# Four graph layers in fp32: where the next group's H and 1/D, single additions and output-projection products stand around layer 1's attention

## The chip, the cores and the metric

The kernel runs on one core of a Trainium2 chip. The metric is the device time of one execution, in microseconds. Below, PE is TensorE (matmul), DVE is VectorE, ACT is ScalarE, POOL is GpSimd and SP is SyncE, which issues most of the DMAs.

## The reference

The input x holds 128 graphs of 64 nodes with 512 features, adj holds their weighted adjacency matrices. Four layers follow each other; each adds its result to x and normalizes the rows.

```python
# layer 0: hypergraph convolution twice, 512 -> 1024 -> 512
H = (adj != 0); w = adj[:, 0, :]
Dinv = 1 / (H @ w);  Binv = 1 / H.sum(axis=1)
conv(z, W, b) = Dinv * (H @ (Binv * (H^T @ (z @ W^T)))) + b
x = LN(x + conv(layer_norm(relu(conv(x, W1, b1))), W2, b2) + x)
# layer 1: attention from one score per node
s = (x @ w) @ a
A = leaky(8 * tanh((s_i + s_j) / 8)); A = exp(A) * adj
A = A / A.sum(-1) * adj.sum(-1)
x = LN(x + A @ x @ w)
# layer 2: three graph convolutions; layer 3: attention with 8 heads
x = LN(x + adj @ (relu(adj @ (relu(adj @ (x @ gW1) + gb1) @ gW2) + gb2) @ gW3) + gb3)
x = LN(x + heads(softmax(q k^T / 8) * LA + LG * adj + LD * exp(-adj), v) @ Wout + b_out)
```

## The kernel before, in words

**Groups and pairs.** Two graphs fill the 128 partitions and make a pair; G = 4 pairs make a group of 512 rows, and there are 16 groups. All is fp32. A matmul of 128x256 appears twice in the profile for each one in the program.

**Products.** `multiply` (L546) makes a product of 512 rows by 512 columns by Strassen's way (in Winograd's form) with seven products of half size instead of eight. `product` (L528) issues one of them: 8 matmul records, or 16 where the inner size is 1024 (layer 0's W2). Their order is B11, T1, T2, B21, T3, B22, T4. B11, T2, T3 and T4 accumulate in the PSUM tile `pa` (in the profile a_ and the product's key: a_l2c, a_wo), T1 and B22 in `pc` (b_l2c, b_wo), B21 in `pb` (c_l2c, c_wo). After B11, T1 and T2 a copy of the sum so far is taken (`snap`, L555: u1, u5 and u2, all shown as u_l2c and so on); ACT takes it where there is no residual, DVE where there is one. Four additions make the result: L574 after B21 (quarter 0,0), L580 after T3 (1,1), L589 after B22 (0,1), and L598 (a copy on ACT) or L600 after T4 (1,0). T3 accumulates into `pa`, which the copy u2 reads, and T4 into `pa`, which L580 reads. There are four accumulators of this kind (`ps_acc`, bufs=4), so a new tile takes the place of one that an addition has emptied. `sums` (L514) makes the left sides of the seven products on DVE (s_h, s_l and so on); the differences of weights (T1 to T4) are made once, at group 0 (`make`, L263 to L268), and kept in DRAM.

**A group's stages.** `prepare` (L628) makes H and 1/D of a group: ht (H transposed, L633), its row sums db (L635), hn (L641), deg (L642), rowsum (L643), H times the weights and its sums (L660, L661), the inverses inv (L649 to L651), then rb, 1/D turned along the rows (`along`, one transpose of L618 and four of L622), hb (L670), and with PE's sps the matrix smat; cs (L705) is D times degree. `first_half` (side a) is layers 0 and 1 of a group: products l0w1, graph products l0h, product W2 (l0w2), layer norm, the scores and e (`along` again), t = e + s (L817), tanh (L819), exp (L821), tn (L823), den (L828), its turn rd, t (L832), then the products gt_l of x and t, and l1w. `second_half` (side b, and later t) is layer 2 (l2a, l2b, gth, l2c with the result g3, the aggregation agg, L1138, with its additions L1144, the layer norm and xtp, the turned x) and layer 3 (q, k, dot, v, softmax, pv, wo). `first_group` is group 0's own first half, with plain products by rows.

**Order.** The generators of three groups run interleaved: in step n side a works on group n, side b on group n - 1, t on group n - 2. `order` (L1385) lists the stages of one step by hand, `step_1` is step 1's list, `step_last` step 16's, `start` group 0's. Within that list a scheduler orders each engine's instructions by when it takes them to be ready; in group 0 and at the very end the written order is kept (`strict`). `behind(key)` (L501) ties an instruction behind a noted one on the same engine: `last_add` notes additions (`wo_5.d` is the addition L580 of wo of group 5), PE's products (`l2c_5.p5` is the end of T3) and others (`e_5` is t = e + s, `t_5` the finished t, L832). The program's order on an engine is the order in which it runs there.

**Weights.** `Stream` loads each product's weights into a ring of 20 tiles as earlier ones come free. A group's adj is loaded more than a step ahead.

Of the kernel before, what the change touches and what calls it, by code (L numbers as in the profile page):

```python
# [10 lines left out]
AF = mybir.ActivationFunctionType  # L11
# [30 lines left out]
def kernel(  # L42
# [286 lines left out]
    w_o = Weight(Wout, 0, "wo")  # L329
# [166 lines left out]
    last_add = {}  # L496
# [4 lines left out]
    def behind(key):  # L501
        return tc.issue_after(last_add[key]) if key in last_add else nullcontext()
# [40 lines left out]
                )  # L543
        stream.done(*wt_q, what)

    def multiply(lefts, wt_q, dst, key, flipped=False, res=None, stops=(3,), then=None, held=None):  # L546

        acc = [ps_acc.tile([P, 2, Q], FP, name=f"{n}_{key}", tag="acc") for n in "ab"]

        def snap(ps, m, n, what):
            t = work.tile([P, 2, Q], FP, name=f"{what}_{key}", tag="w")
            last_add[f"{key}.{what}"] = (act.copy(t, ps) if res is None else vec.tensor_add(t, ps, res(m, n))).ins  # L555
            return t

        pa, pc = acc
        product(pa, lefts, wt_q, B11, True, False, flipped)
        s1 = snap(pa, 0, 0, "u1")  # L560
        if 1 in stops:
            yield
        product(pc, lefts, wt_q, T1, True, False, flipped)
        s5 = snap(pc, 1, 1, "u5")
        if 2 in stops:
            yield
        product(pa, lefts, wt_q, T2, False, False, flipped)
        s2 = snap(pa, 0, 1, "u2")
        last_add[f"{key}.p3"] = newest(PE)
        if 3 in stops:  # L570
            yield
        pb = ps_acc.tile([P, 2, Q], FP, name=f"c_{key}", tag="acc")
        product(pb, lefts, wt_q, B21, True, True, flipped)
        vec.tensor_add(dst(0, 0), pb, s1)  # L574
        if then:
            then(0, 0, dst(0, 0))
        if 4 in stops:
            yield
        product(pa, lefts, wt_q, T3, False, False, flipped)
        last_add[f"{key}.d"] = vec.tensor_add(dst(1, 1), pa, s5).ins  # L580
        if then:
            then(1, 1, dst(1, 1))
        last_add[f"{key}.p5"] = newest(PE)
        if 5 in stops:
            yield
        product(pc, lefts, wt_q, B22, False, True, flipped)
        last_add[f"{key}.p6"] = newest(PE)
        with behind(held):
            last_add[key] = vec.tensor_add(dst(0, 1), pc, s2).ins  # L589
        if then:  # L590
            then(0, 1, dst(0, 1))
        if 6 in stops:
            yield
        product(pa, lefts, wt_q, T4, False, True, flipped)
        if then:
            then(1, 0, pa)
        elif res is None:
            act.copy(dst(1, 0), pa)  # L598
        else:
            vec.tensor_add(dst(1, 0), pa, res(1, 0))  # L600

    def whole(gen):
        for _ in gen:
            pass

    def nat(t):

        return lambda m, n: t[:, 2 * m : 2 * m + 2, n * Q : (n + 1) * Q]
# [19 lines left out]
    def prepare(g):  # L628
# [24 lines left out]
        if q == 0:  # L653
            inverse(inv[:, 1], db[:, 1])
        else:
            by_rows()
            if q > 2:
                yield
            with behind(f"agg_{q - 2}") if q > 2 else nullcontext():
                vec.tensor_mul(hn[:, 1], hn[:, 0], g["wb"])  # L660
                vec.reduce_sum(db[:, 0], hn[:, 1], axis=AX.X)  # L661
                inverse(inv, db)
        cs = small.tile([P, G], FP, name=f"cs_{q}", tag="cs")
        g["cs"], g["rowsum"] = cs, rowsum
        if q > 0:

            rb = grp.tile([P, G, C], FP, name=f"rb_{q}", tag="rb", bufs=1)
            along(rb, inv[:, 0])
        hb = grp.tile([P, G, C], FP, name=f"hb_{q}", tag="hb", bufs=1)
        vec.tensor_mul(hb, ht, bcast(inv[:, 1], G))  # L670
        yield
# [64 lines left out]
    def first_half(g):  # L736
# [79 lines left out]
        t = grp.tile([P, G, C], FP, name=f"t_{q}", tag="t", bufs=1)  # L816
        last_add[f"e_{q}"] = vec.tensor_add(t, e, bcast(s4, G)).ins  # L817
        yield "w2"
        act.activation(t, t, AF.Tanh, scale=0.125)  # L819
        vec.scalar_tensor_tensor(t, t, 0.1, t, ALU.mult, ALU.max)  # L820
        last_add[f"exp_{q}"] = act.activation(t, t, AF.Exp, scale=8.0).ins  # L821
        tn = grp.tile([P, G, C], FP, name=f"tn_{q}", tag="tn", bufs=1)
# [73 lines left out]
    def first_group(g):  # L896
# [107 lines left out]
        out_of_2(0, rows_of(0, hts, w2))  # L1004
        yield "w20"
        out_of_2(1, rows_of(1, hts, w2))
        scored(0)
        yield "w21"
        ps = rows_of(2, hts, w2)
        yield "w22"  # L1010
        attention(0)
# [2 lines left out]
        ps = rows_of(3, hts, w2, 0, 1)  # L1014
        yield "w23"
        out_of_2(3, rows_of(3, hts, w2, 1, 2, ps))
        scored(1)
        stream.used(w_2)
        yield "w24"
        left = Left("l1_0")  # L1020
        graph_T(pair, t, left.t, 0, "l1_0")
        yield "c30"
        mvs = [small.tile([P, 2, 2], FP, name=f"mv_l1_0_{d}", tag="mvp") for d in range(2)]

        def out_of_l1(p):
# [29 lines left out]
    def second_half(g):  # L1055
# [62 lines left out]
        h2.sums()  # L1118
        yield "gh"
        g3 = big.tile([P, G, D], FP, name=f"g3_{q}", tag="big")  # L1120
        gen = multiply([h2], (w_g[2], q), nat(g3), f"l2c_{q}", stops=(3, 5), held=f"t_{q + 1}")
        next(gen)
        yield "l2c1"
        with behind(f"e_{q + 1}"):
            next(gen)
        yield "l2c2"
        with behind("exp_1") if q == 0 else nullcontext():
            whole(gen)
        yield "l2c"
        for duo in range(2):  # L1130

# [67 lines left out]
            taken(1, ps, left)  # L1199
        left.sums()  # L1200
        yield "osum"
        for n, _ in enumerate(multiply([left], (w_o, q), nat(xg), f"wo_{q}", res=nat(xg), stops=(1, 3))):
            yield f"o{n + 1}"
        yield "o"
        with behind(f"q_{q + 1}"):
            o = out[q * T : (q + 1) * T, :].rearrange("(p t) d -> t p d", t=P)
# [165 lines left out]
    def taken(duo, ps, left):  # L1372
# [6 lines left out]

    start = """  # L1380
        a0.c1 prep0 keep0 rest a0.w1a keep1 a0.w1b rows0 bw0 a0.c20 wa bw0 a0.c21 doubled0 constant0 rows1 a0.w20 keep2 wa
        a0.w21 prep1 a0.w22 a0.ss0 a1.c1 a0.w23 doubled1 a0.w24 a0.c30 a1.w1a1 a0.l10 a0.ss1 a0.l11 a1.w1a2
        a0.c31 a1.w1a keep3 a1.resid a0.l12 a1.w1b1 a0.l13 a1.w1b2 b0.gt a1.w1b
    """.split()
    order = """  # L1385
        t.v1 a.c1 t.v b.gt t.soft a.w1a1 a.w1a t.soft2 a.resid b.l2a1 b.l2a a.w1b1 t.ptp a.w1b t.pv a.lnh b.l2b1
        t.osum a.c2a b.l2b a.c2b b.gb3 load a.w21 b.gh a.w2 rows b.l2c1 b.l2c2 a.ss a.den b.l2c t.o1 t.o2 a.c3 b.agg rows2 t.o
        a.p1 b.xT a.p2 b.q1 a.ln1 b.q t.ln3 b.k1 prep b.k b.dots
    """.split()

    step_1 = """
        b.l2a1 b.l2a a.lnh b.l2b1 a.c2a b.l2b a.c2b b.gb3 load a.w21 b.gh a.w2 b.l2c1 b.l2c2 a.ss sumsq b.l2c a.den b.agg
        sumsq2 a.c3 a.p1 b.xT sumsk a.p2 b.q1 a.ln1 b.q b.k1 rows b.k prep b.dots
    """.split()

    step_last = """
        t.v1 b.gt t.v t.soft t.soft2 b.l2a1 t.ptp b.l2a t.pv t.osum b.l2b1 b.l2b b.gb3 b.gh b.l2c1 b.l2c2 b.l2c t.o1 b.agg
        t.o2 t.o b.xT b.q1 b.q t.ln3 b.k1 b.k b.dots
    """.split()
    rest_last = "t.v1 t.v2 t.v t.pv0 t.o1 t.pv1 t.o".split()  # L1400
    orders = {1: step_1, NGRP: step_last, NGRP + 1: rest_last}
# [43 lines left out]
    for n, (who, q, name) in enumerate(todo):  # L1445
        if n == n_start:
            strict.clear()
        if n == n_end:
            strict.update((PE, DVE))
        if who == "load":  # L1450
            if q > 1:
                groups[q] = load_group(q)
        elif who == "rows":
            if q > 0:
                preps[q] = prepare(groups[q])
            with behind(f"l0w2_{q - 1}" if q > 2 else "q_0") if q > 1 else nullcontext():
                next(preps[q])
        elif who in ("prep", "rows2"):
            next(preps[q])
        elif who == "doubled":  # L1460
            doubled(groups[q])
        elif who == "constant":
            constant(groups[q])
        elif who == "keep":
            wt = (*w_1, w_2, w_l1)[q]
            stream.keep(wt)
        elif who == "wa":
            if isinstance(wa_parts, tuple):
                wa_parts = make_wa(*wa_parts)
                vec.tensor_copy(mcol, mcol8)  # L1470
                vec.tensor_copy(mi, mi8)
            else:
                spread_wa(wa_parts)
        elif who == "rest":
            with in_turn(SP, POOL):
                wa_parts = load_wa()
                b2_bc = load_row(b2, D, "b2_bc")
                groups[1] = load_group(1)
                load_atx(first)
                load_masks(first)  # L1480
                load_masks_cols()
                gb1_col = load_col(gb1, KD, "gb1_col")
                gb2_col = load_col(gb2, KD, "gb2_col")
                gb3_bc = load_row(gb3, D, "gb3_bc")
                bo_bc = load_row(bout, D, "bo_bc")
        elif who in ("sumsq", "sumsq2"):
            stream.make_half(w_q)
        elif who == "sumsk":
            stream.make(w_k, 0)
        elif who == "bw":  # L1490
            next(bw_parts)
        else:
            side = "a" if who == "a" else "b"
            if (side, q) not in gens:
                gens[side, q] = (second_half if side == "b" else first_half if q > 0 else first_group)(groups[q])
            did = next(gens[side, q])
            assert did == name, (did, name)
# [55 lines left out]
```

## Time and profile before

| | |
|---|---|
| runs | 2763.16 us median of 3 (2761.98 to 2764.21) |
| the profiled execution | 2763.43 us, its span 2761.7 us |
| PE busy | 2726.4 us, 99% |
| DVE busy | 2074.4 us, 75% |
| ACT busy | 801.8 us, 29% |
| share of DMA engines, hardware queue | 46.9% |
| step 3, from b_wo to b_wo (525.0 to 694.8) | 169.8 us, PE busy 168.78, DVE 128.79 |
| group 0 (0 to 140) | PE busy 132.69 |

Busy times overlap and do not add up. In the timeline an entry is start, length, engine, line, operation, output and inputs, shape, count; a bracket at the end is the engine's idle time before it and what ended that. Matmuls overlap each other, so a sum of starts tells more than idle time. The granted clock of TensorE was 1.000.

### The profile page before, as it was taken

To read this page: it belongs to the slowest core of one execution; us is meant where nothing else is said; L and a number is where in the kernel's file an instruction comes from. 1 tells how busy PE (TensorE), PEld (TensorE's weight loads), DVE (VectorE), ACT (ScalarE), POOL (GpSimd) and SP (SyncE) were. 2 spreads that over 40 slices of the span, in tenths; PEclk is the share of its full clock that TensorE was granted. 3 is DMA by queue.
4 is the path that set the end of the run, shared out by engine and by line. 5 is a ranking of instruction groups with operands and counts; after the bars stand their busy time and mean duration, and the time that the engine had idled before them with its cause. 6 is when DMAs were issued, how large, how long until landed. Compare 5 with 4: busy or idle time off the path is not lost.

```text
span 2761.7 us, 67726 instructions
## 1 busy us (share of the span) xinstructions
PE 2726.4 (99%) x28770; PEld 2346.2 (85%) x28770; DVE 2074.4 (75%) x4117; ACT 801.8 (29%) x1444; POOL 37.6 (1%) x71
## 2 busy tenths in 40 slices
PE   9999999999999999999999999999999999999998
PEld 7888888888888888888888888888888888888887
DVE  6878687776877778777786877778777687776766
ACT  3323223233232322322223232232322323132232
POOL 2000000000000000000000000000000000000000
PEclk9999999999999999999999999999999999999999
DMA  8535454454544545445454454545545455454541
GB/s 267 170 116 160 131 164 139 139 164 132 168 130 138 166 133 162 130 142 165 132 164 128 143 164 132 162 127 149 161 130 166 132 153 152 125 164 131 153 124 61
DMA packets 309389, 405.14 MB, mean 147 GB/s; under 512 B 57409, under 2 KB 185185, under 8 KB 309089
## 3 DMA queue, kind: packets, MB, share of 16 engines
q1 hardware_dynamic: 304256, 385.58, 46.9%
q0 software_dynamic: 4832, 15.24, 1.5%
q8 instruction: 228, 3.74, 0.6%
q14 instruction: 73, 0.59, 0.1%
HBM read 369.78 MB, written 30.93 MB: 145 GB/s over the span
## 4 chain that ended last, share of the span: by engine, by line
PE 85%; DVE 13%; issue 1%; ACT 1%; DMA 0%; DVEq 0%
PE a_l0w L539 13%; PE b_l0w L539 7%; PE a_l2b L539 4%; PE a_l2a L539 4%; PE a_v L539 4%; PE c_l0w L539 4%; PE a_k L539 4%; PE a_q L539 4%; PE a_l1w L539 3%; PE gt_l L481 3%; PE a_l2c L539 2%; PE gt_l0h L481 2%; PE a_wo L539 2%; PE b_l2b L539 2%; PE b_l1w L539 2%; PE b_l2a L539 2%
## 5 line engine op out<-in xcount | busy, mean ns | idle before, releaser
L539 PE MATMUL a_l0w<-w2w,aT_l0h 128*128 128x256 f32 x720 | 164.3, 381 | 0.0
L457 DVE BATCH_NORM_STATS2 st_l<-x 128x6 f32<-128x512 f32 x244 | 157.3, 670 | 0.1
L539 PEld LDWEIGHTS a_l0w<-w2w,aT_l0h 128*128 128x128 f32 x720 | 135.6, 190 | 18.8
L463 DVE TENSOR_SCALAR x<-x,mv_l,rs_l 128x512 f32<-128x512 f32 x244 | 119.1, 540 | 1.8
L539 PE MATMUL b_l0w<-w2w,s_l0h 128*128 128x256 f32 x480 | 108.5, 379 | 0.0
L766 ACT ACTIVATE h<-h 128x1024 f32<-128x1024 f32 (+1 forms) x58 | 54.9, 947 | 178.5 <-DVE h L589 157.5
L539 PEld LDWEIGHTS b_l0w<-w2w,s_l0h 128*128 128x128 f32 x480 | 91.1, 190 | 12.5
L1112 ACT ACTIVATE aT_h<-gth,gb_col 128x256 f32<-128x256 f32 x128 | 48.5, 490 | 159.0 <-PE gth L1104 159.0
L447 ACT ACTIVATE rs_l<-mv_l,eps_t 128x4 f32<-128x4 f32 (+1 forms) x64 | 19.0, 297 | 257.6 <-DVE mv_l L458 245.8
L555 DVE TENSOR_TENSOR u_l0w<-a_l0w,b_bc 128x512 f32<-128x512 f32 x56 | 38.5, 688 | 69.3 <-PE a_l0w L539 69.3
L492 ACT COPY aT_l<-gt_l 128x512 f32<-128x512 f32 x148 | 78.2, 597 | 40.0 <-PE gt_l L481 39.9
L539 PE MATMUL a_l1w<-ww,aT_l 128*128 128x256 f32 x360 | 87.3, 379 | 0.2 <-ACT aT_l L492 0.2
L539 PE MATMUL a_l2b<-gwbw,aT_h 128*128 128x256 f32 x360 | 86.6, 383 | 0.7 <-ACT aT_oT L1375 0.7
L539 PE MATMUL a_wo<-wow,aT_oT 128*128 128x256 f32 x336 | 80.7, 383 | 6.1 <-DVE x L580 6.1
L539 PE MATMUL a_q<-aT_xT,wqw 128*128 128x256 f32 x360 | 85.1, 379 | 0.7 <-ACT aT_xT L1163 0.7
L539 PE MATMUL a_l2c<-gwcw,aT_h 128*128 128x256 f32 x360 | 85.3, 380 | 0.0
L539 PE MATMUL a_k<-aT_xT,wkw 128*128 128x256 f32 x360 | 85.0, 379 | 0.0
L539 PE MATMUL a_l2a<-aT_l,gwaw 128*128 128x256 f32 x360 | 85.0, 379 | 0.0
L539 PE MATMUL a_v<-wvw,aT_xT 128*128 128x256 f32 x336 | 80.8, 383 | 0.0
L539 PE MATMUL a_l0w<-w1aw,aT_l 128*128 128x256 f32 x336 | 80.8, 383 | 0.0
L539 PE MATMUL a_l0w<-w1bw,aT_l 128*128 128x256 f32 x336 | 79.4, 379 | 0.0
L539 PEld LDWEIGHTS a_wo<-wow,aT_oT 128*128 128x128 f32 x336 | 62.8, 190 | 19.4 <-DVE x L580 10.9
(528 smaller groups left out, 6491.2 us busy)
## 6 DMA issues: line engine op xcount, KB each, us to landing
w2w<-w2k SPq DMA_DIRECT2D x210, 256.0 KB, 2.7
x<-in_x_dram SPq DMA_DIRECT2D x15, 1024.0 KB, 5.7
w1aw<-w1ak SPq DMA_DIRECT2D x60, 256.0 KB, 2.6
w1bw<-w1bk SPq DMA_DIRECT2D x60, 256.0 KB, 2.7
ww<-wk SPq DMA_DIRECT2D x60, 256.0 KB, 2.7
gwaw<-gwak SPq DMA_DIRECT2D x60, 256.0 KB, 3.0
gwbw<-gwbk SPq DMA_DIRECT2D x60, 256.0 KB, 2.6
gwcw<-gwck SPq DMA_DIRECT2D x60, 256.0 KB, 2.6
```

The costliest lines, as they stand in the source:

```text
L447: act.activation(rs[:, at], mv[:, at, 1], AF.Sqrt, bias=eps_t)
L457: vec.bn_stats(st, xg[:, p, :])
L463: vec.tensor_scalar(xg[:, p, :], xg[:, p, :], mv[:, p, 0:1], rs[:, p : p + 1], ALU.subtract, ALU.mult)
L481: ten.matmul(ps[g][f * C : (f + 1) * C, c, p, :], src(2 * duo + p)[rows, c0 : c0 + C], mat[rows, 2 * duo + p, :], start=True, stop=True,)
L492: act.copy(o[:, :, :, g, :], ps[g])
L539: ten.matmul(acc[:, blk, :], lhsT, rhs, start=(first and blk == 0 and i == 0), stop=(last and i == n_k - 1), skip_group_check=True,)
L555: last_add[f"{key}.{what}"] = (act.copy(t, ps) if res is None else vec.tensor_add(t, ps, res(m, n))).ins
L766: act.activation(hn, hn, AF.Relu)
L1112: act.activation(o[:, :, h, :], ps[h][:, c].rearrange("p (d a) i -> p d (a i)", d=2), AF.Relu, bias=gb2_col[:, k : k + 1],)
```

## The change

- `prepare`: its first part (ht, db, hn, deg, rowsum) is tied behind W2's addition L580 of the group ahead (`l0w2_{q-1}.d`) instead of its last addition, and stands before side b's l2c1 in step 1 too. In group 2 the second part is tied as the first was before. Then comes a stop, and rb is tied behind L580 of the output projection of three groups before (`wo_{q-3}.d`); hb is not tied.
- `multiply`: `held` is now a table. In l2c the addition after B21 is tied behind `e_{q+1}` and the one after B22 behind `t_{q+1}`; before, all that followed the first stop up to T3 was traced behind `e_{q+1}`. In group 0 the tie behind `exp_1` goes, and `a.den` stands before `b.l2c` in step 1.
- Output projection: one stop more (after T1), and its second and third product are tied behind l2c's T3 and T4 of the next group.
- In group 1 the tanh is tied behind l2c's copy u2 of group 0.
- Group 0: `scored(0)` comes after the next group's smat, `scored(1)` after the first graph product of layer 1.

```diff
-    def multiply(..., then=None, held=None):
+    def multiply(..., then=None, held={}):
...
-        vec.tensor_add(dst(0, 0), pb, s1)
+        with behind(held.get(4)):
+            vec.tensor_add(dst(0, 0), pb, s1)
...
-        with behind(held):
+        with behind(held.get(6)):
             last_add[key] = vec.tensor_add(dst(0, 1), pc, s2).ins
...
+        last_add[f"{key}.p7"] = newest(PE)
...
-            if q > 2:
+            if q > 1:
                 yield
-            with behind(f"agg_{q - 2}") if q > 2 else nullcontext():
+            with behind(f"agg_{q - 2}" if q > 2 else "q_0") if q > 1 else nullcontext():
...
+            if q > 2:
+                yield
             rb = grp.tile([P, G, C], FP, name=f"rb_{q}", tag="rb", bufs=1)
-            along(rb, inv[:, 0])
+            with behind(f"wo_{q - 3}.d"):
+                along(rb, inv[:, 0])
...
-        act.activation(t, t, AF.Tanh, scale=0.125)
+        with behind("l2c_0.u2") if q == 1 else nullcontext():
+            act.activation(t, t, AF.Tanh, scale=0.125)
...
         out_of_2(1, rows_of(1, hts, w2))
+        yield "w21"
         scored(0)
-        yield "w21"
+        yield "sc0"
...
-        scored(1)
         stream.used(w_2)
         yield "w24"
...
         yield "c30"
+        scored(1)
+        yield "sc1"
...
-        gen = multiply([h2], (w_g[2], q), nat(g3), f"l2c_{q}", stops=(3, 5), held=f"t_{q + 1}")
+        gen = multiply([h2], (w_g[2], q), nat(g3), f"l2c_{q}", stops=(3, 5),
+            held={4: f"e_{q + 1}", 6: f"t_{q + 1}"})
         next(gen)
         yield "l2c1"
-        with behind(f"e_{q + 1}"):
-            next(gen)
+        next(gen)
         yield "l2c2"
-        with behind("exp_1") if q == 0 else nullcontext():
-            whole(gen)
+        whole(gen)
...
-        for n, _ in enumerate(multiply([left], (w_o, q), nat(xg), f"wo_{q}", res=nat(xg), stops=(1, 3))):
-            yield f"o{n + 1}"
+        gen = multiply([left], (w_o, q), nat(xg), f"wo_{q}", res=nat(xg), stops=(1, 2, 3))
+        next(gen)
+        yield "o1"
+        for n in range(2):
+            with behind(f"l2c_{q + 1}.p{5 + 2 * n}"):
+                next(gen)
+            yield f"o{n + 2}"
+        whole(gen)
...
-            with behind(f"l0w2_{q - 1}" if q > 2 else "q_0") if q > 1 else nullcontext():
+            with behind(f"l0w2_{q - 1}.d") if q > 1 else nullcontext():
                 next(preps[q])
```

In the lists of stages `start` gets a0.sc0 and a0.sc1, `order` gets t.o3 and rows3, `step_1` has rows before b.l2c1, rows2 before b.k1 and a.den before b.l2c, and `step_last` gets t.o3.

## The prediction

> **What bounds the kernel now.** I read the page's first part, then TensorE's (PE's) table of waits, then the timeline around the two longest waits that repeat.
>
> ```profile
> span 2761.7 us, 67726 instructions
> PE 2726.4 (99%) x28770; PEld 2346.2 (85%) x28770; DVE 2074.4 (75%) x4117; ACT 801.8 (29%) x1444; POOL 37.6 (1%) x71
> ```
>
> PE is the bound: 2761.7 - 2726.4 = 35.3 us of the span are not matmul. The change removes no matmul, so only PE's waiting can be won, and any time that DVE saves counts only where PE waits for DVE.
>
> ```profile
> PE b_wo L539 <- DVE g L574: 6.8, 13, 1.1
> PE a_wo L539 <- DVE x L580: 6.6, 13, 0.5
> ...
> PE a_l2c L539 <- ACT u_l2c L555: 1.8, 1, 1.8
> ```
>
> Two waits come 13 times each, once per step 2 to 14 (a step is one turn of the order, about 169.8 us). The first of them, in step 8:
>
> ```profile
> 1372.86 1.89 PE L539 MATMUL b_l2c<-gwcw,s_h 128*128 128x256 f32 x8
> ...
> 1374.15 0.43 DVE L817 TENSOR_TENSOR t<-e,s 128x256 f32<-128x256 f32 x1
> 1374.49 0.68 DVE L574 TENSOR_TENSOR g<-c_l2c,u_l2c 128x512 f32<-128x512 f32 x1
> 1374.61 0.42 ACT L819 ACTIVATE t<-t 128x256 f32<-128x256 f32 x1 [4.83 <-DVE t L817]
> ...
> 1374.93 0.57 ACT L555 COPY u_l2c<-a_l2c 128x512 f32<-128x512 f32 x1
> ...
> 1375.23 1.13 PE L539 MATMUL b_wo<-wow,s_oT 128*128 128x256 f32 x4 [0.48 <-DVE g L574]
> ```
>
> A product of 8 matmuls takes 1.73 us of PE (a_l2c starts at 1371.13, b_l2c at 1372.86). So the next was due at 1374.59; b_wo needs the bank that VectorE's (DVE's) L574 empties, and that addition stands behind L817. It starts 0.64 late and its first four matmuls take 0.97 instead of 0.86, 0.11 more: **0.75 us lost**, though the table of waits calls it 0.48 (overlap of matmuls hides the rest).
>
> ```profile
> 1389.84 1.89 PE L539 MATMUL b_wo<-wow,s_oT 128*128 128x256 f32 x8
> 1389.87 0.45 DVE L618 STREAM_TRANSPOSE rb<-inv 128x256 f32<-128x256 f32 x1
> 1390.24 0.38 DVE L670 TENSOR_TENSOR hb<-ht,inv 128x256 f32<-128x256 f32 x1
> ...
> 1390.64 1.25 DVE L622 STREAM_TRANSPOSE rb<-inv 32x128 f32<-32x128 f32 x4
> ...
> 1391.92 0.69 DVE L580 TENSOR_TENSOR x<-a_wo,u_wo 128x512 f32<-128x512 f32 x1
> ...
> 1392.67 0.48 PE L539 MATMUL a_wo<-wow,aT_oT 128*128 128x256 f32 x1 [0.51 <-DVE x L580]
> ```
>
> The second: a_wo's last product (T4) waits for L580, whose input (T3 of a_wo) was done at 1390.00, but which stands behind the turning of 1/D (rb). Due at 1391.99 after two a_l1w matmuls, it starts at 1392.67, and takes 1.83 instead of 1.73: **0.78 lost**.
>
> Step 15 prepares no further group: H and rb are missing from it, the rest is the same. It is a ready experiment:
>
> ```profile
> 2561.45 1.89 PE L539 MATMUL b_l2c<-gwcw,s_h 128*128 128x256 f32 x8
> ...
> 2562.18 0.42 DVE L817 TENSOR_TENSOR t<-e,s 128x256 f32<-128x256 f32 x1
> ...
> 2562.96 0.57 ACT L555 COPY u_l2c<-a_l2c 128x512 f32<-128x512 f32 x1
> ```
>
> From the start S of b_l2c's second product, L817 begins at S+0.73 here and at S+1.29 in step 8; u_l2c ends at S+2.08 here, S+2.64 there. There b_wo is only 0.08 late, and a_wo's T4 not at all.
>
> **What the Trainium skill says.** "PSUM — Partial Sum Buffer", Engine vs sequencer instructions: ScalarE's (ACT's) and DVE's queues are strict FIFO, matmuls start in program order. The trace agrees: a_l2c's T2 ended at 1373.02, but its copy u_l2c stood behind the tanh until 1374.93. "Perfetto Trace Analysis", Optimization Strategy: the same gap over and over on the saturated engine can mean too few PSUM buffers. It fits the first wait (four accumulators, b_wo needs c_l2c's), not the second. "ScalarE: Activation LUTs", What ACT_TABLE_LOAD costs: 1283 ns, 2.66 us with its drain. The trace has the 1.28 but no drain: in step 8 a load begins at 1398.38, 0.02 after a copy, and the root runs at 1399.67.
>
> **The change, part by part** (order of instructions as the changed program has them, durations from step 8).
>
> *H into W2.* Five DVE instructions (ht 0.28, hn 0.26, db 0.39, deg 0.39, rowsum 0.41: 1.73 in all) go behind W2's addition L580 of the group ahead. In the hole there
>
> ```profile
> 1357.52 0.69 DVE L580 TENSOR_TENSOR x<-a_l0w,u_l0w 128x512 f32<-128x512 f32 x1 [2.76 <-PE a_l0w L539]
> 1360.18 0.69 DVE L518 TENSOR_TENSOR s_h<-aT_h 128x512 f32<-128x512 f32 x1 [1.97 <-PE b_l0w L539]
> ```
>
> they end by 1359.6 (1358.12 plus starts 0.2 to 0.33 apart plus the last's 0.41), so nothing waits; adn and atc are loaded a group ahead. The layer norm behind it then runs as in step 15, 0.56 earlier. Without that cover it would cost up to 1.73.
>
> *Additions and projection products one by one.* PE's order was B22 of l2c, half of b_wo, T3 of l2c; it becomes B22, T3, six matmuls of b_wo, T4, the rest. b_wo no longer stands first; T3 does, and it needs u_l2c, still behind the tanh from step 3 on. With step 15's timing u_l2c ends at S+2.08, PE follows 0.06 later (as at 192.74 in step 1, after a copy that ended at 192.68): T3 at S+2.14, due at S+1.73: 0.41 + 0.10 = 0.51 lost instead of 0.75, **a gain of 0.24**. What is late next: T4 needs the addition L580 of g3, on DVE behind den at S+4.31, done S+5.0; PE comes to T4 at S+2.14 + 0.10 + 1.73 + 6 x 0.216 = S+5.27. It just fits. t is ready at S+7.3, its products come at S+9.2.
>
> *1/D in two parts.* rb and its four blocks go behind L580 of wo; only hb (0.38) stays ahead. L580 then runs from 1390.17 to 1390.86, T4 is due at 1391.57: **the 0.78 are gone**. rb's 1.7 us now lie before the addition L589 at about 1392.55 (1392.53 before); a_l1w and its sums have a slack of 1 us. The next check is the layer norm for xtp (L1158): PE comes 0.78 earlier, at 1402.45; its pairs 0 and 1 are ready at about 1401.6, pairs 2 and 3 at 1402.5 for use at 1403.05. It fits by some 0.5.
>
> *Steps 1 and 2.* Here u_l2c goes ahead of the tanh and T3 does not wait (1.8 + 0.2 won in step 1). But in step 1 g3's addition L589 now stands behind t and one weight difference: t ends at about 196.85, L589 at 198.05; the aggregation, which needs it, then takes 2.6 us, so the next turn comes at 200.7 instead of 199.25: net 1.4 lost. Later H no longer delays kT's addition: the 0.6 wait with its overlap, 0.7, goes. In step 2 four weight differences (0.6 each) move ahead of t; DVE reaches the addition for T4 at S+4.05, T4 waits 1.4, where before b_wo lost 1.2 and more: 0.1 won, and the second wait's 0.78.
>
> *Group 0's two places.* S (smat) ahead of the score takes 0.8 of PE's wait for it (gt_l on smat), aT_l ahead of the root 0.5 (pp on aT_l), with overlap 1.5. The score's root still starts at 86.76, since it waits for statistics that end at 86.73. DVE runs through from there to 98.40 without PE, so W1's next product on a_l0w, due at 98.2, waits 0.3 for the copy that ends then: 1.2 won.
>
> *The queues of DMA.* On SP one adn load changes places with a weight's, which is asked for long before its use; on POOL nothing moves.
>
> *Step 15* loses 0.51 - 0.19 = 0.3 by T3's new place.
>
> **Sum:** -1.2 + 1.4 - 0.7 - 0.9 - 12 x (0.24 + 0.78) + 0.3 = -13.3 us. The profiled execution took 2763.43 (span 2761.7); that gives 2750.1, and against the median of the runs, 2763.16, 2749.9. I say 2750.
>
> **Unknown sizes.** The first wait's gain lies between -0.32 (norm no earlier: u_l2c at S+2.64, 1.07 lost) and +0.75 (no wait); taken 0.24, since step 15 shows that very timing. Over 12 steps this is 2757 to 2744. Steps 1 and 2 together: -3 to +3, taken -0.2.
>
> **Rivals.**
> 1. *The first wait vanishes too*, were u_l2c ready by S+1.67. Step 15 speaks against it. 2744. Chance 0.10.
> 2. *Given back at xtp*: the layer norm behind rb is late and eats the 0.78. For it: DVE is 75% busy. Against: the 0.5 of slack worked out. Then -13.3 + 13 x 0.78 = -3.2: 2760. Chance 0.08.
> 3. *Slower: T3 at the head of PE's queue.* If the tanh's table load falls between t and u_l2c, T3 starts 1.28 later: 1.79 lost instead of 0.75, 0.26 more than the second wait gives back: 12 x 0.26, 1.3 more in step 15 and -1.1 for the ends make about 2766. With the skill's 2.66 a step loses 1.64 net: about 2784. It turns slower once u_l2c ends after about S+3.1. For it: the load stands behind u_l2c in the new steps 1 and 2. Against: from step 3 on ACT's order is as before, the load in 4.83 us of idle time. Chance 0.05.
> That the change does nothing is excluded by the order of instructions.
>
> **How the numbers follow.** The sum's case has 0.77. The range 2744 to 2757 holds it with its bounds and rival 1; rivals 2 and 3 (0.13) are left out. A measurement here tells 0.2%, 5.5 us, from no change: faster 0.88, same 0.08 (rival 2), slower 0.04 (most of rival 3).
>
> **What would show it.** Right: no wait a_wo on x L580; b_wo on g L574 gone, in its place a_l2c on ACT u_l2c some 0.25 each, 13 times; in step 1 agg waiting for g L589 by some 3 us; H's lines ending before s_h. Wrong: a wait xtp on x (rival 2), a_l2c waits above 1 us (rival 3), or none (rival 1).

## Result, and the profile after

The changed kernel took 2749.28 us (median, 2748.92 to 2751.61), the kernel before 2763.53 (2761.98 to 2764.21): a ratio of 0.9951, 95% interval 0.9934 to 0.9968. The prediction said 2750, so the time was right. It was right in the 12 equal steps to a hundredth of a us each, and in the start and steps 1 and 2 by errors that cancel, as shown below.

The head of the page of the changed kernel:

```profile
span 2747.5 us, 67717 instructions
PE 2722.5 (99%) x28770; PEld 2347.5 (85%) x28770; DVE 2079.6 (76%) x4117; ACT 803.3 (29%) x1444; POOL 38.1 (1%) x71
```

The matmuls are as many as before, and what is not matmul fell from 35.3 to 25.0 us (2747.5 - 2722.5). PE's busy time fell by 3.9 as well, since part of a wait is counted as busy there: at T3 below the first matmul after the wait has a record of 0.48 us, the others 0.38.

TensorE's table of waits of the changed kernel (us in total, times, longest):

```profile
PE a_l2c L539 <- ACT u_l2c L555: 3.2, 13, 0.3
PE agg L1145 <- DVE g L590: 2.8, 1, 2.8
PE a_l2c L539 <- DVE g L581: 1.5, 2, 1.0
```

Both waits that came 13 times are gone, b_wo on g and a_wo on x. In place of the first stands a shorter one, T3 of l2c on u_l2c. The aggregation's wait in step 1 is new. Step 8 around T3, from the timeline of the changed kernel (a count at the end covers what lies in the window that was asked for). Line numbers have moved: the additions L574, L580 and L589 are L575, L581 and L590, t = e + s (L817) is L822, the tanh (L819) L825, ht (L633) L635, rowsum (L643) L645, rb's turn (L618) L620, hb (L670) L675, the aggregation (L1138) L1145 and its additions (L1144) L1151.

```profile
1365.64 1.89 PE L539 MATMUL b_l2c<-gwcw,s_h 128*128 128x256 f32 x8
...
1366.37 0.42 DVE L822 TENSOR_TENSOR t<-e,s 128x256 f32<-128x256 f32 x1
...
1366.83 0.42 ACT L825 ACTIVATE t<-t 128x256 f32<-128x256 f32 x1 [4.29 <-DVE t L822]
1367.15 0.57 ACT L555 COPY u_l2c<-a_l2c 128x512 f32<-128x512 f32 x1
...
1367.77 1.56 PE L539 MATMUL a_l2c<-gwcw,aT_h 128*128 128x256 f32 x6 [0.25 <-ACT u_l2c L555]
```

With S = 1365.64: L822 begins at S+0.73, the copy ends at S+2.08, T3 starts at S+2.13. It was due at S+1.73, so it is 0.40 late, and its first matmul takes 0.10 more until the next one starts (0.32 instead of 0.22). That is step 15's timing of before, now in every step. The second place of the same step:

```profile
1382.38 1.89 PE L539 MATMUL b_wo<-wow,s_oT 128*128 128x256 f32 x8
1382.42 0.42 DVE L675 TENSOR_TENSOR hb<-ht,inv 128x256 f32<-128x256 f32 x1
1382.76 0.68 DVE L581 TENSOR_TENSOR x<-a_wo,u_wo 128x512 f32<-128x512 f32 x1
...
1383.36 0.43 DVE L620 STREAM_TRANSPOSE rb<-inv 128x256 f32<-128x256 f32 x1
...
1384.11 1.67 PE L539 MATMUL a_wo<-wow,aT_oT 128*128 128x256 f32 x7
```

L581 ends at 1383.44, 0.67 ahead of T4, where before it ended after T4 was due; rb follows it. And H, in the hole of W2:

```profile
1350.30 0.69 DVE L581 TENSOR_TENSOR x<-a_l0w,u_l0w 128x512 f32<-128x512 f32 x1 [2.76 <-PE a_l0w L539]
1350.91 0.28 DVE L635 TENSOR_SCALAR ht<-atc 128x256 f32<-128x256 f32 x1
...
1351.96 0.41 DVE L645 TENSOR_REDUCE rowsum<-adn 128x4 f32<-128x256 f32 x1
1352.96 0.69 DVE L518 TENSOR_TENSOR s_h<-aT_h 128x512 f32<-128x512 f32 x1 [0.59 <-PE b_l0w L539]
```

The five instructions end at 1352.37, and VectorE still waits 0.59 for TensorE before s_h: the cover held.

The period, from one start of c_wo to the next, is 168.75 to 168.77 us in the repeating steps, against 169.77 before, but for single steps in which PE halts inside a group of small matmuls (the profile calls it "issue"; more of that at the end).

### The profile page after: what moved, and what is told of

Its sections match the earlier page's. It is cut to its first block, busy times and chain, and to the rows that moved or that the text cites. A ratio compares the mean times of both kernels' runs of the same rounds, so it can differ in the third digit from the quotient of the medians.

```text
span 2747.5 us, 67717 instructions
## 1 busy us (share of the span) xinstructions
PE 2722.5 (99%) x28770; PEld 2347.5 (85%) x28770; DVE 2079.6 (76%) x4117; ACT 803.3 (29%) x1444; POOL 38.1 (1%) x71
## 4 chain that ended last, share of the span: by engine, by line
PE 88%; DVE 10%; ACT 1%; issue 1%; POOL 0%; DVEq 0%; POOLq 0%
PE a_l0w L539 13%; PE b_l0w L539 7%; PE a_l2b L539 4%; PE a_q L539 4%; PE a_k L539 4%; PE a_l2a L539 4%; PE a_v L539 4%; PE c_l0w L539 4%; PE a_l1w L539 4%; PE gt_l L481 3%; PE a_wo L539 3%; PE gt_l0h L481 2%; PE a_l2c L539 2%; PE b_l2b L539 2%; PE b_q L539 2%; PE b_k L539 2%
## 5 line engine op out<-in xcount | busy, mean ns | idle before, releaser
L539 PEld LDWEIGHTS b_l0w<-w2w,s_l0h 128*128 128x128 f32 x480 | 91.1, 190 | 12.5
L539 PEld LDWEIGHTS a_l2c<-gwcw,aT_h 128*128 128x128 f32 x360 | 67.0, 190 | 18.7 <-ACT u_l2c L555 8.7
```

Of the source, the lines that this page charges most:

```text
L539: ten.matmul(acc[:, blk, :], lhsT, rhs, start=(first and blk == 0 and i == 0), stop=(last and i == n_k - 1), skip_group_check=True,)
```

## The experiments

The medians are of 4 to 21 executions. The ratios of e1 to e8 are to executions of the kernel before that were timed along with them (median 2763.33). Three further kernels, e9 to e11, are one execution each and stand in the text. The period is that of the undisturbed steps 3 to 14, from one trace of each kernel.

| kernel | median us | ratio to before, 95% | period us |
|---|---|---|---|
| before | 2763.5 | | 169.77 |
| changed | 2749.28 | 0.9951 (0.9934 to 0.9968) | 168.76 |
| e1 H back | 2757.47 | 0.9978 (0.9969 to 0.9986) | 169.32 |
| e2 no product ties | 2745.76 | 0.9937 (0.9924 to 0.9949) | 168.45 |
| e3 rb back | 2760.23 | 0.9988 (0.9982 to 0.9995) | 169.54 |
| e4 g3 free in step 1 | 2747.23 | 0.9942 (0.9928 to 0.9955) | 168.76 |
| e5 before, with H alone | 2756.76 | 0.9975 (0.9965 to 0.9985) | 169.22 |
| e6 group 0 back | 2752.54 | 0.9961 (0.9947 to 0.9974) | 168.77 |
| e7 e2 and e4 together | 2743.24 | 0.9929 (0.9916 to 0.9941) | 168.44 |
| e8 e7, u_l2c early | 2746.16 | 0.9937 (0.9925 to 0.9950) | 168.59 |

**H back in the layer norm** (e1):

```
-            with behind(f"l0w2_{q - 1}.d") if q > 1 else nullcontext():
+            with behind(f"l0w2_{q - 1}" if q > 2 else "l0w2_1.d") if q > 1 else nullcontext():
                 next(preps[q])
```

> The changed kernel with one part undone: from step 2 on, H's five VectorE instructions stand again in the layer norm in front of the first product's addition. Theory (T3's stall is set by u_l2c, behind the tanh, and H's place sets when the tanh comes): L822 begins 0.56 us later after b_l2c's start, T3 of l2c idles about 0.8 instead of 0.25 and loses 1.07 instead of 0.51 in each of 12 steps, the step takes 169.3 instead of 168.8 us, the whole 2749.3 + 12 x 0.56 = 2756. Rival (the gain of the first wait comes from the new order of products and H's place is worth nothing, since H fell into VectorE's idle time before as after): 2749, T3 idle unchanged at 0.25.

In its timeline, step 8, T3 waits 0.80 where it waited 0.25:

```profile
1372.28 1.56 PE L539 MATMUL a_l2c<-gwcw,aT_h 128*128 128x256 f32 x6 [0.80 <-ACT u_l2c L555]
```

The period is 0.56 longer, as the theory had it, so H's place is worth 0.56 a step although H ran on an engine with idle time before and after. The median is 1.5 above the sum. The trace has one more wait in step 2 (gt_l on t, 0.5), and three of its periods are longer than 169.32, by 1.5 in all, where one of the changed kernel's is longer, by 0.5; these are the "issue" halts.

**The projection's products untied** (e2):

```
-            with behind(f"l2c_{q + 1}.p{5 + 2 * n}"):
-                next(gen)
+            next(gen)
```

> The changed kernel with one part undone: the projection's second and third product are no longer tied behind l2c's, so half of b_wo stands again ahead of T3 of l2c; H and 1/D stay at their new places. Theory (with H early, b_wo needs only the bank of c_l2c, which step 15 of the kernel before got 0.08 late, so this order loses 0.19 a step where the tied one loses 0.51): a_l2c's wait on u_l2c goes, b_wo waits 0.1 or less on g, the step takes 168.45 instead of 168.77, the whole 2749.3 - 13 x 0.32 = 2745. The part of the change named 'products tied one by one' would then cost time by itself. Rival (the tie is what removes the first wait): b_wo waits 0.48 again and loses 0.75, the step 169.0, the whole 2752.

The period is 168.45, and a_l2c's wait on u_l2c is gone from the table. Tying the products one by one costs 0.31 a step by itself: it puts T3, which needs the copy u_l2c behind the tanh, ahead of b_wo, which needs only the accumulator that L575 empties, and with H early L575 comes in time. Step 8 of e2:

```profile
1366.02 1.89 PE L539 MATMUL b_l2c<-gwcw,s_h 128*128 128x256 f32 x8
1367.09 0.68 DVE L575 TENSOR_TENSOR g<-c_l2c,u_l2c 128x512 f32<-128x512 f32 x1
1367.83 1.13 PE L539 MATMUL b_wo<-wow,s_oT 128*128 128x256 f32 x4
```

Here S is 1366.02; b_wo starts at S+1.81, 0.08 late, with 0.10 more in its first matmul.

**rb ahead of the projection's addition** (e3):

```
-            if q > 2:
-                yield
             rb = grp.tile([P, G, C], FP, name=f"rb_{q}", tag="rb", bufs=1)
-            with behind(f"wo_{q - 3}.d"):
-                along(rb, inv[:, 0])
+            along(rb, inv[:, 0])
```

(with `rows3` out of the order)

> The changed kernel with one part undone: the turning of 1/D (rb and its four blocks) stands again ahead of the projection's second addition. Theory (the second wait is that turning and nothing else): a_wo waits on x 0.5 us 13 times again and loses 0.78 each, the step takes 169.55 us, the whole 2749.3 + 13 x 0.78 = 2759.4. Rival (part of what the first wait gave is absorbed here, because the second wait is fixed by VectorE's own chain): the second wait grows to 0.78 + 0.24 = 1.02 a step, 2762.6. Other rival (given back at xtp, so that the place of rb is worth less): 2753 or less.

The table of waits of e3 has both:

```profile
PE a_wo L539 <- DVE x L581: 6.6, 13, 0.5
...
PE a_l2c L539 <- ACT u_l2c L555: 3.2, 13, 0.3
```

169.54 - 168.76 = 0.78, neither 1.02 nor less. The second wait does not absorb what the first gives, because VectorE's work ahead of it starts from TensorE's own aggregation (its first addition, L1148 in e3, waits 0.25 for agg; from there to L581 VectorE runs without a break) and so moves with it.

**H alone on the kernel before** (e5). The edit is one word, `.d`, at the place of e1; TensorE's order is that of before.

> The kernel before with one part of the change alone: from group 3 on, H's five VectorE instructions stand behind W2's second addition; TensorE's and ScalarE's orders are those of before. Theory (H in the layer norm is the whole of the first wait except 0.19): b_wo's wait on g falls from 0.48 to 0.1 or less in 12 steps, the step takes 169.2 instead of 169.77, the whole 2763.3 - 12 x 0.56 = 2756.6; the wait of a_wo on x stays 0.5, 13 times. Rival (H's place pays only together with T3's new place): the step stays at 169.77, 2763.

From its table of waits:

```profile
PE a_wo L539 <- DVE x L580: 6.7, 13, 0.5
...
PE b_wo L539 <- DVE g L574: 0.5, 1, 0.5
```

b_wo waits once, in step 2, instead of 13 times. With e1, e2 and the two kernels themselves this gives the first wait in all four combinations. A step without either wait is 168.76 - 0.51 = 168.25, with the 0.51 lost at T3 (0.40 late and 0.10 in its first matmul, by the rounded times above); the loss is what each period has above that (less 0.78 where rb is at its old place):

| | products not tied | products tied |
|---|---|---|
| H in the layer norm | 0.74 (before) | 1.07 (e1) |
| H in W2 | 0.19 (e5), 0.20 (e2) | 0.51 (changed) |

H gives 0.55 or 0.56 in each column, the ties take 0.31 to 0.33 in each row. They add. And e5 has the old ties of l2c's own additions, e2 the new ones; their losses are the same to 0.01, so tying those additions one by one is worth nothing to this wait.

**Group 0's last addition free in step 1** (e4):

```
-            held={4: f"e_{q + 1}", 6: f"t_{q + 1}"})
+            held={4: f"e_{q + 1}", 6: f"t_{q + 1}" if q > 0 else None})
```

> The changed kernel with one line changed in step 1 alone: the last addition of group 0's g3 (L590) no longer stands behind t and a weight difference, but right behind tn. Theory (the 2.77 us that the aggregation idles, and the granted clock of 0.59 that follows it from 196.4 to 200.5, both come from that one place): the idle time falls below 0.7, the clock stays near 1.00, and the aggregation and its turn take 0.96 and 0.34 less; with t itself 0.7 later, which may leave gt_l a wait of up to 0.5, a gain of 2.5 to 4: 2746. Rival (the aggregation would wait anyway, for its banks or for t): gain 1 or less, 2748.5 and more, with another wait of 1.5 to 2.5 in the same 10 us.

The aggregation no longer waits and the clock stays at 1.00 there. By the medians the gain is 2.1, less than the theory's 2.5 to 4 and more than the rival's 1. Counted from gth, a_l1w comes 4.1 us earlier than in the changed kernel, but xtp only 2.8: between them 1.3 went back, most of it in a new wait. The timelines of e4 show it (TensorE's, then that of all engines):

```profile
201.63 1.97 PE L539 MATMUL b_l1w<-ww,s_l 128*128 128x256 f32 x8 [1.11 <-issue]
```

```profile
199.65 0.68 DVE L267 TENSOR_TENSOR wqt<-wqb,wqb 128x512 f32<-128x512 f32 x1
200.25 0.68 DVE L268 TENSOR_TENSOR wqt<-wqb,wqt 128x512 f32<-128x512 f32 x1
200.85 0.68 DVE L518 TENSOR_TENSOR s_l<-aT_l 128x512 f32<-128x512 f32 x1
```

The profile names no releaser, but b_l1w multiplies s_l, whose first part L518 ended at 201.53, 0.10 before. It stood behind two weight differences of 0.6 each. So part of the gain seems to have gone into VectorE's queue. That reading is from the trace; the differences were not moved to try it.

**Group 0's two places back** (e6, and once more without a further edit, e11): `scored(0)` ahead of "w21", `scored(1)` ahead of "w24" again.

> The changed kernel with one part undone: group 0's score and the layer norm after its attention's second half stand again at their old places (DVE's and ACT's orders alone). Theory: gt_l waits again for smat and pp for aT_l, and the products from 166 us on start later by what these two places brought, 1.7 us by the two traces (1.2 by the sum of the prediction), 2751. Rival (these two waits are only shifted, and the wait for W1's copy hides the gain): the start differs by less than 0.5, 2749.5.

> The kernel with group 0's places back once more, without a further edit. Its start differed from the changed kernel's by 1.74 us, its time by 3.3. Theory (the places bring 1.7, the rest are short stalls of PE inside gt_l that the profile puts to 'issue', 1.8 us in that trace against 0.3): the start lags by 1.7 again, and the 'issue' stalls have another size. Rival (the stalls belong to this order of instructions): 1.8 us again at the same place; the aggregation's start to xtp 12.9 us again, or 14.5 by the theory of the clock.

Layer 2's first graph products of group 0 (gth) start 1.76 and 1.77 us later than in the changed kernel, counted from group 0's first turning (gt_l0h). The time of e11, 2752.23, is 1.5 and 1.9 above those of e9 and e10, the changed kernel on the same chip (2750.69 and 2750.29). The median of e6 is 3.3 above that of the changed kernel; the "issue" halts in gt_l were 1.8 us in e6 and 0.7 in e11, at the same place. Their size doesn't belong to this order of instructions, and it makes comparisons of 1 or 2 us by single times unsafe. The places bring 1.8, by the start of gth.

**The clock in step 1** (e9 and e10 are the changed kernel without an edit):

> The changed kernel once more, without any edit. In its trace the aggregation of step 1 starts after 2.77 us of idle PE and the granted clock is 0.50 for 3.4 us from there; with the same 2.77 us the clock stayed at 1.00 in two of the kernels with one part undone (H back, group 0's places back), where the aggregation started 1.2 and 1.9 us later. Theory (the clock falls when a window of the throttle, which runs free of the program, happens to lie in the idle time): the same program shows the drop in some executions and not in others, the path from the aggregation's start to xtp taking 14.5 us with it and 12.9 without. Rival (it depends on the program's place alone): 14.5 us and 0.50 again in each execution of this program.

> The changed kernel a third time, without any edit; expected as for the second: 14.5 us from the aggregation's start to xtp by the rival, 14.5 or 12.9 by the theory.

From the aggregation's start to xtp took 14.55 us in the changed kernel, 14.50 and 14.57 in its repeats: three times the same, as the rival had it. The pair of e6 and e11 tells them apart, one program in two executions: 12.89 and 14.49. The stretches behind the same wait of 2.77 us, from the answers by windows (us, PE busy, PEld, DVE, ACT, POOL, then the granted clock, DMA share, GB/s), first the changed kernel, then e6, then e11:

```profile
196.40:199.40 3.00, 3.00 (x17) 0.95 (x21) 1.83 (x3) 0.00 (x0) 0.72 (x2) 0.59 0.46 175
```

```profile
198.26:200.02 1.76, 1.76 (x16) 0.66 (x20) 1.16 (x3) 0.00 (x0) 0.71 (x2) 1.00 0.39 149
```

```profile
198.77:201.50 2.73, 2.73 (x16) 0.92 (x20) 1.24 (x3) 0.00 (x0) 0.72 (x2) 0.50 0.50 192
```

Some 16 recorded matmuls took 1.76 us at full clock and 2.73 at half. By slices of 1 us the clock of the changed kernel was 0.96, 0.50, 0.50, 0.50, 0.84 from 196 to 201, which is half clock for 3.4 us. The wait ahead of it:

```profile
195.66 0.68 DVE L590 TENSOR_TENSOR g<-b_l2c,u_l2c 128x512 f32<-128x512 f32 x1
196.40 0.64 PE L1145 MATMUL agg<-g,atc 64*64 64x512 f32 x1 [2.77 <-DVE g L590]
```

The drop was there in six of eight traces with this wait, and missing in e1 and e6. The record of the clock in the traces shows what decides. In each of the 13 traces the record begins with full clock 8.75 to 12.02 us after the span's start, and there the small matmuls' records shorten (from 0.31 to 0.22 us in the changed kernel). Each later fall, that at the end of the program too, comes a whole number of stretches of 3.413 us after that rise, to 0.001 of a stretch. In step 1 it is 55 stretches, in all six. So these stretches lie on a grid that is fixed within an execution and lies differently to the program in each. (The start feels it as well: gt_l0h begins at 42.12 with the rise at 9.18, at 42.73 with 10.88 in e11, and at 43.30 with 12.02 in e1.) The eight traces, by the stretch that holds most of the wait (us):

| trace | clock rises | stretch | PE idle | idle within the stretch | clock falls |
|---|---|---|---|---|---|
| changed | 9.18 | 193.50 to 196.92 | 193.63 to 196.40 | 2.77 | 196.92 |
| e2 | 10.21 | 194.53 to 197.95 | 193.97 to 196.74 | 2.21 | 197.95 |
| e3 | 9.03 | 193.35 to 196.76 | 193.69 to 196.45 | 2.76 | 196.76 |
| e9 | 9.82 | 194.14 to 197.56 | 193.83 to 196.60 | 2.46 | 197.56 |
| e10 | 8.97 | 193.29 to 196.70 | 193.68 to 196.45 | 2.77 | 196.70 |
| e11 | 10.88 | 195.20 to 198.61 | 196.00 to 198.77 | 2.61 | 198.61 |
| e1 | 12.02 | 192.93 to 196.34 | 194.83 to 197.60 | 1.51 | no |
| e6 | 9.70 | 194.02 to 197.44 | 195.49 to 198.26 | 1.95 | no |

After a stretch with 2.21 us of idle PE or more the next one ran at half clock; after none with 1.95 us or less did it, in any of the 13 traces from the rise to the last matmuls. Between these two nothing was measured. In e1 and e6 the wait lay across a border of two stretches, so that neither had enough. That settles the question of e9 for the theory: the same wait can halve the clock or not, and the three repeats were alike because all three waits fell well inside one stretch. With a wait of 2.77 us and a stretch of 3.413, limits of 1.95 and 2.21 give an estimate of two thirds to a half of all executions with the drop.

"TensorE: Matmul & The Clock Gate" in the Trainium skill, Part 1: The HAM clock gate, says that the clock halves after an idle window of about 3.4 us, and that this window runs free and does not restart with the kernel. The 3.4 us and the free grid agree; but a window did not have to be idle as a whole, 2.21 us of it were enough here.

**Two versions beyond the change.** e7 has the edits of e2 and e4. e8 also drops `4:` from `held`, so that L575 stands ahead of L822; the copy u_l2c then goes ahead of the table load and the tanh in every step, and T3 stands inside b_l2c.

> The changed kernel without the projection's ties and with group 0's L590 right behind tn. Theory (the two are at different places of PE's order and add): 2745.8 - 2.2 to 3.3 = 2743, the step 168.45, no wait of agg on g. Rival (they share slack in step 1): 2745.

> As the one before, and the first addition of l2c (L575) is not held behind L822 either: it stands ahead of it, u_l2c's copy goes ahead of the table load and the tanh in every step, and T3 of l2c stands inside b_l2c's product, ahead of all of b_wo. Theory (the 0.19 that is still lost is b_wo's bank, and t has a slack of 1.9 us): the tanh comes 1.1 us later, neither T3, T4 nor b_wo waits, the step takes 168.26 instead of 168.45, the whole 2741. Rival (the table load of 1.28, now between the copy and the tanh, delays L826 and with it T4's addition or t): a wait of a_l2c on g or of gt_l on t of 0.2 or more a step, 2744 or more.

e7 did what was expected: 2743.24, the fastest of all, and its edits add: they were worth 3.5 and 2.1 alone, and are worth 6.0 together. e8 did not: its period is 168.59, 0.15 longer than e7's. T3 no longer waits, but its own result does, as the timeline of step 8 shows:

```profile
1366.86 0.69 DVE L581 TENSOR_TENSOR g<-a_l2c,u_l2c 128x512 f32<-128x512 f32 x1 [0.70 <-PE a_l2c L539]
...
1367.61 1.99 PE L539 MATMUL a_l2c<-gwcw,aT_h 128*128 128x256 f32 x8
```

Only the second half of b_l2c, four matmuls or 0.86 us, lies between T3 and T4, while T3's last matmul, its addition and the semaphore take until 1367.61; T4 was due at 1367.45. It loses 0.16 and 0.10 more in its first matmul, and T3 itself 0.08 at its start, 0.34 in all against 0.19 at b_wo in e7. The rival was right that T4's addition comes late, wrong in the cause: VectorE sat idle for 0.70 us ahead of L581, waiting for T3; the table load delayed nothing.

## Why the prediction was right

- **First wait, -0.24 a step.** Held: T3 loses 0.51 instead of 0.75. Of this H gives 0.56 and the ties take about 0.32, as e1, e2 and e5 show; the 1.07 of e1 is the prediction's own bound for a norm that comes no earlier. The working took the sum of both and did not say that one part of the change loses.
- **Second wait, -0.78 a step.** Held to the hundredth (e3). T4 starts when due.
- **H in the hole.** Held: ended 0.59 before s_h.
- **xtp.** Held: its pairs 2 and 3 end at 1395.00, needed at about 1395.6, half way through its 1.22 us; rival 2 did not occur. Nor did rival 3: the tanh starts 0.04 after L822, its load is long done. T3 was 0.25 idle, not above 1.
- **Steps 3 to 15.** Their sum was -12 x 1.02 + 0.3 = -11.9, and with step 2's second wait -12.7. From the start of c_wo in step 2 to that of step 15 the traces have -13.5 (2207.91 to 2194.42); 1.0 of it are "issue" halts that were shorter in that execution (two steps of 171.04 and 169.98 before, one of 169.26 after), so -12.5 is the change's.
- **The start, -1.2, was mis-sized.** The traces have -1.7 (e6: 1.76). W1's copy costs 0.27, near the 0.3; but the three waits that stood as 1.35 in the table were worth 2.0, not 1.5. Each cost more beyond its entry than was added for it.
- **Step 1, +1.4, was mis-sized.** From gth to xtp the shift went from -1.7 to +0.50, so 2.2 were lost. L590 ended just where worked out (198.05 by the clock of before; 196.34 and 1.72 make 198.06). Two terms behind it were wrong, in opposite ways. The aggregation was taken at 2.6 us, about what its two halves take in the kernel before (194.66 to 195.67, and 197.59 to 199.25):

```profile
194.66 0.64 PE L1138 MATMUL agg<-g,atc 64*64 64x512 f32 x1
197.59 0.64 PE L1138 MATMUL agg<-g,atx 64*64 64x512 f32 x1
199.25 2.14 PE L481 MATMUL gt_l<-t,x 64*64 64x64 f32 x128
```

But the second half waits there for a copy of g (L598); in one piece the aggregation takes 1.8 at full clock (e1: 197.60 to 199.37), so that only 0.6 would be lost, as in e6. And the clock was put in at full, without a word; at half it takes 3.0 (196.40 to 199.39), and the turn behind it slows as well, 1.6 more in all (e11 against e6). The failed step is this term that was put at nothing: the wait's length was foreseen, not that it halves the clock. That the two errors leave only 0.8 is luck, and where the grid of the clock stood in the execution is luck too.

- **kT, -0.7, and step 2's start, -0.1**, measured about -0.9 and -0.2.

From the start to c_wo of step 2 the terms were to make -1.2 + 1.4 - 0.7 - 0.1 = -0.6, and the trace has 366.40 to 365.77, -0.6. The errors of -0.5, +0.8 and -0.3 cancel there; that part was right by luck.

## What to carry to other kernels

Work moved out of a queue pays at the next instruction that the saturated engine waits for, even where the engine that did it had idle time: ask what stood behind it. When a change has several parts on one wait, cost each alone, since a part may lose what another has won: here the order of products was tied around a late bank that H's move had already freed. Don't price a stall of the matmul engine by its idle time alone: here each short one cost 0.26 us beyond its entry, and one of 2.77 us cost 1.6 more where it halved the clock. Which is the better to remove first, one long or many short ones, has to be added up.

## What was not expected of the hardware

The 2.77 us of idle TensorE were followed by 3.4 us at half clock in six executions of eight, 1.6 us of loss each, whereas shorter idle times, up to 1.83 us (an "issue" halt of e6), left the clock at 1.00. Across all traces what tells the two apart is the idle time within one stretch of a 3.413 us grid that starts with the clock's rise: 2.21 us and more, the clock fell, 1.95 and less, it didn't.

A stall costs more than its entry in the table of waits: 0.25 of idle time was 0.51 lost, 0.80 was 1.07, 0.48 was 0.75, which is 0.26 or 0.27 more each time, whatever its length. Of this 0.10 is the slower first matmul, and 0.16 is overlap: a record lasts 0.38 us, and the next matmul normally starts 0.22 after it.

In each execution PE halts for 0.3 to 1.8 us at one or two places inside the long groups of small gt_l matmuls, and the profile names no releaser. The places are three, around 590, 1265 and 1939 us, four steps apart; which of them halt, and how long, changes from one execution to the next. The DMA records of the traces point to the instructions themselves: in all 15 halts above 0.25 us of the 13 traces a 16 KB transfer of the queue that the profile calls "instruction" (q8, 228 transfers in each trace) landed 1.3 to 1.6 us before the halt ended. It landed from 1.2 us ahead of the halt's start (changed kernel, a halt of 0.27) to 0.4 behind it (e6, a halt of 1.83), and the end followed at the same distance. By chance, about one halt in forty would find a landing in so narrow a stretch (228 x 0.3 of 2750 us). These groups also use up instructions fastest, 128 matmuls and 128 weight loads in 2.1 us, against 8 and 8 in 1.73 in a product. So PE most likely waits there for a late block of its program; no run moved such a block to try it, and why these three places is open. The halts are of the size of this change's smaller terms.
